# An edge-message layer on one core: two POOL iotas behind every third scatter, from slot 4 to slot 191

## The chip, the cores and the metric

The kernel runs on one core of one Trainium2 chip. The metric is the device time of one execution in microseconds (us). A core has five engines with a queue of instructions each: PE (matrix multiplication), DVE (vector), ACT (scalar, activation), POOL (GpSimd) and SP, which here issues nearly all plain DMA transfers. POOL issues the indirect DMA transfers.

## The reference, cut to what matters

There are 6250 nodes and 100000 edges with 128 features each. Row `src` of an edge is its own node, `dst` its neighbour; the edges come sorted by `dst`.

```python
msg_in = jnp.concatenate([x[row], x[col], edge_attr], axis=-1)
h = msg_in @ W + b
mu = jnp.mean(h, axis=-1, keepdims=True)
var = jnp.mean(jnp.square(h - mu), axis=-1, keepdims=True)
h = (h - mu) * jax.lax.rsqrt(var + LN_EPS) * gamma + beta
msg = jax.nn.relu(h)
out = jax.ops.segment_sum(msg, row, num_segments=x.shape[0])
# edge_index = [src, dst]; the result is _layernorm(x + out)
```

The sum goes by `src`, while the edges lie in the order of `dst`. So the kernel has to bring the rows of one `src` block together, and it does that by writing them, one row for each edge, to computed places in DRAM.

## The kernel before, in words

**Tiles and slots.** The 100000 edges make 782 tiles of 128 edges. Four tiles make a slot `q`, so there are 196 slots (0 to 195). In a slot, PE multiplies the edge features by their part of `W` (L945) and adds the neighbours' projected rows, picked by a one-hot matrix (L962); ACT copies the four finished tiles from PSUM to a row buffer `hs` (L970), and the node number beside them (L971). There are eight such buffers (`HS = 8`), taken in turn: slot `q` uses buffer `q % 8`, so ACT may write it only when the scatters of slot `q - 8` have read it.

**Scatters.** For each tile, POOL issues one indirect DMA (L992), which writes the tile's 128 rows of 528 bytes from `hs` to the places in `place_i` of a DRAM table `sorted`. There are six such tables, one for each part of the edges (`SPLITS`), and 782 scatters in all. From slot 12 on, a scatter also waits for a given matrix product of PE (`TIE`), which spreads a slot's scatters over the next slot. Scatters share eight semaphores in turn (`DMASW0` to `DMASW7`), and each waits for the landing of the scatter eight before it.

**Pairs.** When a part has been scattered, SP loads it back as `hl`, two blocks of 125 nodes at a time (a pair). DVE makes a one-hot matrix of it (L1108), PE turns it (L1120), ACT copies it out (L1124), PE adds the node's own projection (L1147), ACT takes squares and roots (L1156, L1159), DVE scales and cuts (L1171), PE sums by node (L1180), and DVE adds to `acc` (L1198). The pairs of one part are worked on while the next part is scattered.

**The end.** After the last scatter the 25 pairs of the last part remain, and with them the final normalisation, part of which POOL does (L1238, L1239, L1301), and the store.

**Order.** The order on PE, DVE, ACT and SP is written out by hand (`manual_schedule`). POOL's is not while the scatters run: a scheduler places POOL's instructions, and keeps to the dependences between them. A dependence of the kind `NoSync` only orders two instructions, with no semaphore.

The change touches `scatters` (L981 to L1010). It uses `iota_i` (L388), a tile of 128 columns of 32-bit integers that L389 fills once at the start, and that DVE copies to two other tiles (L414, L415); nothing reads it later.

Of the kernel before, what the change touches and what calls it, by code (L numbers as in the profile page):

```python
# [16 lines left out]
P = 128  # L17
# [296 lines left out]
def fast_path(ctx, tc, io, bad_d):  # L314
# [3 lines left out]
    nc = tc.nc  # L318
# [69 lines left out]
    iota_i = const.tile([P, P], I32, name="iota_i")  # L388
# [440 lines left out]
    held = {}  # L829
# [135 lines left out]
    def evict(s, q):  # L965
        t0 = q * PT
        m = min(PT, TILES - t0)
        hs, hp = hs_all[q % HS], held.pop(("hp", q))
        if q > 0:
            nc.scalar.copy(hs[:, :m, 0:D], hp[:, :m, :])  # L970
        nc.scalar.copy(hs[:, :m, D], sloc[:, t0:t0 + m])  # L971
        if q == 0:
            nc.scalar.copy(hs[:, :m, 0:D], hp[:, :m, :])
        waiting.extend((s, q, j) for j in range(m))

    last_scatter = []
    full_scatters = []
    TIE = (12, 196)
    waiting = []

    def scatters(n, tied):  # L981

        total, seen, at = sum(c for _, c in done), 0, []
        for i, c in done:
            seen += c
            while len(at) < n and seen * n >= (len(at) + 1) * total:
                at.append(i)
        done.clear()
        for k, (s, q, j) in enumerate(waiting[:n]):
            t = q * PT + j  # L990
            parts = P if t < TILES - 1 else LAST
            i = nc.gpsimd.indirect_dma_start(  # L992
                out=sorted_d[s][:, :],
                out_offset=bass.IndirectOffsetOnAxis(ap=place_i[:parts, t:t + 1], axis=0),
                in_=hs_all[q % HS][:parts, j, :], in_offset=None,
            )
            last_scatter[:] = [i.ins.name]
            if first_tile[-2] <= t < first_tile[-2] + FULL:
                full_scatters.append(i.ins.name)
            if tied:  # L1000
                tc.add_manual_dep(i.ins, at[k].name, written, reason="rows behind products")
            tc.declare_no_dep(i.ins, group=f"scatter{s}", reason="rows of different edges")
            tc.add_to_no_dep_group(f"scatter{s}", i.ins)
            if t >= first_tile[-2] + FULL:
                tc.declare_no_dep(i.ins, group="halves", reason="see check_full")
                tc.add_to_no_dep_group("behind", i.ins)
            if q < EARLY:
                tc.declare_no_dep(i.ins, group="clear", reason="see check_early")
                tc.add_to_no_dep_group("early", i.ins)
        del waiting[:n]  # L1010
# [314 lines left out]
    for s in range(n_split):  # L1325
        t = first_tile[s]
# [180 lines left out]
    def work(n):  # L1507

        nonlocal n_steps
        for _ in range(n):  # L1510
            for off, step in FLOW:
                i = n_steps - LEAD - off
                if i % 4 or not 0 <= i // 4 < len(pairs):
                    continue
                if step is None:
                    if i // 4 < n_old:
                        load_pair(*pairs[i // 4])
                    continue
                if off == 0:
                    at_work[i // 4] = (Pair if i // 4 < n_old else Unit)(*pairs[i // 4])  # L1520
                step(at_work[i // 4])
            n_steps += 1
# [24 lines left out]
    for s, (n_tiles, _, _, _) in enumerate(SPLITS):  # L1547
        p0, p1 = first_tile[s] // PT, -(-first_tile[s + 1] // PT)
        slots = p1 - p0
        for i in range(slots):  # L1550
            q = p0 + i
# [16 lines left out]
            if q > 2:  # L1568
                evict(s, q)
            if not TIE[0] <= q < TIE[1]:  # L1570
                scatters(len(waiting), False)
            for g in steps_at.pop(q, []):
                run(g)
            work(n - 3)
            if TIE[0] < q < TIE[1]:
                scatters(len(waiting) - PT, True)
# [146 lines left out]
    for key in steps:  # L1723
        if flag is None and starts[key] >= READY["pool"]:
            assert not waiting
            order.enter_context(tc.manual_schedule(engines={mybir.EngineType.Pool}))
            flag = nc.values_load(bad_d[0:1, 0:1], min_val=0, max_val=1 << 20,
                                  skip_runtime_bounds_check_because="a sum of small counts")
        do[key[0]](*key[1:])
        if waiting and key[0] in "KM":  # L1730
            scatters(1, True)
# [6 lines left out]
@with_exitstack  # L1738
def gnn_resnorm_kernel(ctx, tc, io):
    nc = tc.nc  # L1740
    keep = ctx.enter_context(tc.tile_pool(name="keep", bufs=1))
    bad_t = keep.tile([1, 1], I32, name="bad_t")
    with ExitStack() as inner:
        flag = fast_path(inner, tc, io, bad_t)
    with tc.If(flag > 0):
        with ExitStack() as inner:
            general_path(inner, tc, io)
# [244 lines left out]
```

## Time and profile before

| | us |
|---|---|
| time before, median of 3 runs | 1092.25 (1091.75 to 1092.6) |
| the profiled execution's own time | 1092.0 |
| its span, first to last instruction | 1090.2 |
| first scatter starts, last scatter starts | 10.0, 1007.9 |

The profile is of one execution. The page lists for each engine the busy time and its share of the span; its groups of instructions have a row of the form "line engine operation out<-in xcount | busy us, mean ns of one | idle time of the engine just before them, and what ended most of it". The timeline lists instructions by start time with their duration; an idle time before one stands in brackets, with what ended it. "issue" there means that the profile shows nothing that was waited for. Numbers of POOL lines are those of the kernel before.

### The profile page before, as it was taken

How to read it: one execution, taken by the hardware profiler on the slowest of the kernel's cores; microseconds unless marked ns; L12 is line 12 of the kernel's file. 1: busy time of each engine (PE TensorE's matmuls, PEld its weight loads, DVE VectorE, ACT ScalarE, POOL GpSimd, SP SyncE). 2: the span in 40 equal slices, each digit the busy share in tenths (PEclk: the TensorE clock that was granted, in tenths of full speed). 3: DMA queues.
4: the chain of work that ended last, by engine and by line, in shares of the span. 5: the costliest groups of instructions: out<-in, count | busy, mean ns of one | idle time of the engine just before them, and what ended most of it. 6: DMA issues, size and time to landing. Idle time of an engine off the chain costs nothing.

```text
span 1090.2 us, 27196 instructions
## 1 busy us (share of the span) xinstructions
PE 839.6 (77%) x8590; PEld 782.0 (72%) x8590; DVE 876.9 (80%) x2452; ACT 732.4 (67%) x3117; POOL 819.2 (75%) x901
## 2 busy tenths in 40 slices
PE   6366666637887778687787787988879998997995
PEld 5355565527887767587687787988879988896774
DVE  7587998738798888789988876777758887787997
ACT  5133342117666667567666687988879999997796
POOL 7777777777777777777777777777777777777496
PEclk8687797558899898799999998999999999999998
DMA  7899988458787764677877658877859776764572
GB/s 220 263 272 286 303 271 270 147 188 258 227 268 235 237 204 158 222 240 230 266 251 233 188 176 285 284 259 235 259 181 316 231 236 211 229 183 140 151 201 81
DMA packets 127963, 247.92 MB, mean 227 GB/s; under 512 B 47135, under 2 KB 63153, under 8 KB 127813
## 3 DMA queue, kind: packets, MB, share of 16 engines
q1 hardware_dynamic: 101923, 192.81, 58.6%
q0 software_dynamic: 25024, 52.85, 13.5%
q8 instruction: 69, 1.13, 0.4%
q14 instruction: 81, 0.66, 0.2%
q10 hardware_dynamic: 866, 0.46, 0.2%
HBM read 156.23 MB, written 89.80 MB: 226 GB/s over the span
## 4 chain that ended last, share of the span: by engine, by line
PE 28%; DVE 26%; DMA 25%; ACT 13%; issue 5%; SPq 1%; POOL 1%; ACTq 0%; POOLq 0%; DVEq 0%
DMA sorted<-hs,place_i 17%; PE pa L1180 7%; PE hp L945 7%; DVE msg L1171 6%; PE sel L1147 6%; ACT sq L1156 5%; DMA db<-drel_d 5%; DVE sc L695 4%; DVE ohe L1108 3%; ACT sel L1130 3%; ACT ohn L1124 2%; ACT hs L970 2%; PE tr L1120 2%; DVE oh L691 2%; DVE far L714 2%
## 5 line engine op out<-in xcount | busy, mean ns | idle before, releaser
L992 POOL DMA_INDIRECT sorted<-hs,place_i x782 | 757.5, 969 | 241.9 <-issue 88.8
L970 ACT COPY hs<-hp 128x512 f32<-128x512 f32 x194 | 113.0, 583 | 236.3 <-DMA sorted<-hs,place_i 143.3
L1171 DVE SCALAR_TENSOR_TENSOR msg<-sel,rstd,cut 128x128 f32<-128x128 f32 x920 | 260.5, 345 | 8.2
L945 PE MATMUL hp<-w,eT 128*128 128x128 f32 x1548 | 247.2, 310 | 22.4 <-ACT hs L970 19.9
L1147 PE MATMUL sel<-xa,ohn 128*128 128x128 bf16 x2760 | 201.5, 224 | 59.4 <-ACT sel L1130 58.1
L1180 PE MATMUL pa<-msg,ohe 128*128 128x130 f32 x1780 | 239.1, 285 | 5.2 <-DVE msg L1171 2.3
L1156 ACT ACTIVATE sq<-sel 128x128 f32<-128x128 f32 x866 | 227.6, 281 | 18.7 <-PE sel L1147 17.5
L945 PEld LDWEIGHTS hp<-w,eT 128*128 128x128 f32 x1548 | 218.7, 218 | 26.3 <-ACT hs L970 22.6
L1147 PEld LDWEIGHTS <-ohn 128*128 128x128 bf16 x2850 | 183.4, 100 | 71.6 <-issue 52.5
L1180 PEld LDWEIGHTS pa<-msg,ohe 128*128 128x128 f32 x1780 | 217.7, 196 | 9.7 <-PE sel L1147 2.9
L1156 ACT ACTIVATION_READ_ACCUMULATOR sq<-sel 128x1 f32 x866 | 183.4, 212 | 0.0
L1108 DVE TENSOR_TENSOR ohe<-hl,beside 128x1024 f32<-128x1024 f32 (+2 forms) x138 | 138.9, 1007 | 34.2 <-DMA hl<-sorted 33.3
L1130 ACT COPY sel<-hl 128x512 f32<-128x512 f32 (+1 forms) x225 | 127.1, 565 | 35.2 <-DVE msg L1171 29.2
L1124 ACT COPY ohn<-tr 128x1024 bf16<-128x1024 bf16 (+3 forms) x154 | 123.9, 805 | 4.2 <-PE tr L1120 4.1
L934 DVE TENSOR_SCALAR ohd<-db,part_w 128x512 bf16<-128x512 bf16 x192 | 71.6, 373 | 34.3 <-DMA db<-drel_d 26.0
L1120 PE MATMUL tr<-ident_h,ohe 128*128 128x128 bf16 x910 | 76.6, 224 | 19.0 <-DVE ohe L1108 14.2
L1165 DVE RECIPROCAL rstd<-std 128x4 f32<-128x4 f32 (+1 forms) x229 | 39.2, 171 | 59.6 <-ACT std L1159 57.7
L962 PE MATMUL hp<-win,ohd 126*128 126x128 bf16 x770 | 82.5, 234 | 2.8 <-DMA win<-xb_d 2.8
L1198 DVE TENSOR_TENSOR acc<-acc,pa 128x260 f32<-128x260 f32 x123 | 51.6, 419 | 35.3 <-PE pa L1180 34.5
L1120 PEld LDWEIGHTS <-ohe 128*128 128x128 bf16 x910 | 59.1, 100 | 27.8 <-DVE ohe L1108 20.8
L1159 ACT ACTIVATE std<-ss,eps 128x4 f32<-128x4 f32 (+1 forms) x229 | 68.1, 297 | 7.4
L962 PEld LDWEIGHTS <-ohd 126*128 126x128 bf16 x770 | 66.4, 107 | 7.0 <-issue 2.6
(246 smaller groups left out, 862.6 us busy)
## 6 DMA issues: line engine op xcount, KB each, us to landing
eT<-in_eT SPq DMA_DIRECT2D x96, 512.0 KB
hl<-sorted SPq DMA_DIRECT2D x75, 528.0 KB
db<-drel_d SPq DMA_DIRECT2D x96, 256.0 KB
sorted<-empty SPq DMA_DIRECT2D x100, 198.0 KB
sorted<-hs,place_i POOLq DMA_INDIRECT x782
hl<-sorted SPq DMA_DIRECT2D x42, 264.0 KB
hl<-sorted SPq DMA_DIRECT2D x25, 396.0 KB
sorted<-empty SPq DMA_DIRECT2D x50, 132.0 KB
```

What stands on the lines that cost most here:

```text
L945: pe(nc.tensor.matmul(hp[:, j, :], eT[:, at], w[:, 2, :], start=j == 0, stop=False, skip_group_check=True), 4)
L962: pe(nc.tensor.matmul(hp[:, j, :], oh[:3 * WN, at], win[:3 * WN, :], start=False, stop=j == m - 1, skip_group_check=True))
L970: nc.scalar.copy(hs[:, :m, 0:D], hp[:, :m, :])
L992: i = nc.gpsimd.indirect_dma_start(out=sorted_d[s][:, :], out_offset=bass.IndirectOffsetOnAxis(ap=place_i[:parts, t:t + 1], axis=0), in_=h ...
L1108: nc.vector.tensor_tensor(self.ohe[:, :k, :], self.rows()[:, :k, D:D + 1].to_broadcast([P, k, P]), row_bc(iota_p, k), op=ALU.is_equal)
L1120: pe(nc.tensor.transpose(tr[:, j, :], half[:, j0 + j, 1::2], ident_h))
L1124: nc.scalar.copy(self.ohn[:, :self.k, :], self.tr[:, :self.k, :])
L1130: copy(self.sel[g][:, :m, :], self.rows()[:, j0:j0 + m, 0:D])
L1147: pe(nc.tensor.matmul(sel[:, j, :], self.ohn[:, j0 + j, :], xa[:, b, i * D:(i + 1) * D], start=False, stop=j == m - 1 and i == 2, skip_gro ...
L1156: nc.scalar.activation(sq[:, j, :], self.sel[g][:, j, :], AF.Square, accum_out=ss[:, j:j + 1])
L1171: nc.vector.scalar_tensor_tensor(self.msg[:, j0 + j, 0:D], self.sel[g][:, j, :], rstd[:, j:j + 1], cut, op0=ALU.mult, op1=ALU.max)
L1180: pe(nc.tensor.matmul(self.pa[:, h, :], self.ohe[:, j, :], self.msg[:, j, :], start=(j == h), stop=(j == k - 2 + h)), 4)
```

## The change

Behind the scatter of every tile `t` with `t % 3 == 2` in slots 4 to 191, `scatters` issues two iotas on POOL that write 128 columns of `iota_i` in all 128 partitions. Order-only dependences put the first behind that scatter, the second behind the first, and the next scatter in program order behind the second.

```diff
+    PACED = (4, 192)
+    ordered = mybir.DependencyInfo(mybir.DependencyClass.NoSync, mybir.DependencyReason.DATA)
...
         for k, (s, q, j) in enumerate(waiting[:n]):
...
             i = nc.gpsimd.indirect_dma_start(
...
                 in_=hs_all[q % HS][:parts, j, :], in_offset=None,
             )
+            if held.get("pause"):
+                tc.add_manual_dep(i.ins, held.pop("pause"), ordered, reason="behind the pause")
+            if PACED[0] <= q < PACED[1] and t % 3 == 2:
+                last = i.ins.name
+                for _ in range(2):
+                    pause = nc.gpsimd.iota(iota_i, pattern=[[1, P]], base=0, channel_multiplier=0)
+                    tc.add_manual_dep(pause.ins, last, ordered, reason="behind the scatter")
+                    last = pause.ins.name
+                held["pause"] = last
             last_scatter[:] = [i.ins.name]
```

Tiles 17, 20, ... 767 are meant: 251 of them, so 502 iotas. On PE, DVE, ACT and SP the same instructions stand in the same order as before. On POOL the 782 scatters stay, and 502 iotas stand among them: 208 times two in a row, and 86 times one alone.

The usual form is two in a row. Here are POOL's rows near tile 195 (slot 48), before; `sorted1` is the second part's table, `hs0` and `hs1` are row buffers, and the brackets name the semaphores that the instruction waits for: a lane of the scatters' eight, PE's and ACT's.

```order
L992 DMA sorted1_72<-hs0_174,place_i_167 67616x132 [waits DMASW2_49,PE_49]
L992 DMA sorted1_72<-hs0_174,place_i_167 67616x132 [waits DMASW3_49,PE_49]
L992 DMA sorted1_72<-hs1_175,place_i_167 67616x132 [waits DMASW4_49,PE_49,Activation_49]
L992 DMA sorted1_72<-hs1_175,place_i_167 67616x132 [waits DMASW5_49,PE_49]
L992 DMA sorted1_72<-hs1_175,place_i_167 67616x132 [waits DMASW6_49,PE_49]
L992 DMA sorted1_72<-hs1_175,place_i_167 67616x132 [waits DMASW7_49,PE_49]
```

And the same place on POOL in the changed kernel; `x2` is two rows that read alike, and `Pool` is the semaphore that POOL's own instructions count up.

```order
L994 DMA sorted1_72<-hs0_174,place_i_167 67616x132 [waits DMASW2_49,PE_49]
L1004 IOTA iota_i_114 128x128 [waits Pool_49] x2
L994 DMA sorted1_72<-hs0_174,place_i_167 67616x132 [waits DMASW3_49,PE_49]
L994 DMA sorted1_72<-hs1_175,place_i_167 67616x132 [waits DMASW4_49,PE_49,Activation_49]
L994 DMA sorted1_72<-hs1_175,place_i_167 67616x132 [waits DMASW5_49,PE_49]
L1004 IOTA iota_i_114 128x128 [waits Pool_49] x2
L994 DMA sorted1_72<-hs1_175,place_i_167 67616x132 [waits DMASW6_49,PE_49]
L994 DMA sorted1_72<-hs1_175,place_i_167 67616x132 [waits DMASW7_49,PE_49]
```

Two iotas moved in behind every third scatter. All of them write the same tile, and each but the first carries a wait on POOL's own semaphore, for the write of the iota before it.

The other form is rarer. Before, at the turn from slot 45 (`hs5`) to slot 46 (`hs6`) on POOL:

```order
L992 DMA sorted1_72<-hs5_179,place_i_167 67616x132 [waits DMASW4_49,PE_49,Activation_49]
L992 DMA sorted1_72<-hs5_179,place_i_167 67616x132 [waits DMASW5_49,PE_49]
L992 DMA sorted1_72<-hs5_179,place_i_167 67616x132 [waits DMASW6_49,PE_49]
L992 DMA sorted1_72<-hs5_179,place_i_167 67616x132 [waits DMASW7_49,PE_49]
L992 DMA sorted1_72<-hs6_180,place_i_167 67616x132 [waits DMASW0_49,PE_49,Activation_49]
L992 DMA sorted1_72<-hs6_180,place_i_167 67616x132 [waits DMASW1_49,PE_49]
```

And in the changed kernel at that turn:

```order
L994 DMA sorted1_72<-hs5_179,place_i_167 67616x132 [waits DMASW4_49,PE_49,Activation_49]
L1004 IOTA iota_i_114 128x128 [waits Pool_49]
L994 DMA sorted1_72<-hs5_179,place_i_167 67616x132 [waits DMASW5_49]
L994 DMA sorted1_72<-hs5_179,place_i_167 67616x132 [waits DMASW6_49,PE_49]
L1004 IOTA iota_i_114 128x128 [waits Pool_49]
L994 DMA sorted1_72<-hs6_180,place_i_167 67616x132 [waits DMASW7_49,PE_49,Activation_49]
L1004 IOTA iota_i_114 128x128 [waits Pool_49]
L994 DMA sorted1_72<-hs5_179,place_i_167 67616x132 [waits DMASW0_49]
L994 DMA sorted1_72<-hs6_180,place_i_167 67616x132 [waits DMASW1_49,PE_49]
```

Here a scatter stands between the two iotas of a couple, and the last scatter of slot 45 has changed places with the first of slot 46. Five such exchanges of neighbours are all that changes in the order of the 782 scatters.

## The prediction

> **What bounds the kernel now.** I read the page's busy shares first, then POOL's group of scatters, then POOL's timeline.
>
> ```profile
> span 1090.2 us, 27196 instructions
> PE 839.6 (77%) x8590; PEld 782.0 (72%) x8590; DVE 876.9 (80%) x2452; ACT 732.4 (67%) x3117; POOL 819.2 (75%) x901
> ...
> L992 POOL DMA_INDIRECT sorted<-hs,place_i x782 | 757.5, 969 | 241.9 <-issue 88.8
> L970 ACT COPY hs<-hp 128x512 f32<-128x512 f32 x194 | 113.0, 583 | 236.3 <-DMA sorted<-hs,place_i 143.3
> ```
>
> By the shares DVE leads and POOL comes third with 75%. That is misleading. The 782 scatters have 757.5 us of work and 241.9 us of idle time before them, and 241.9 / 782 is 0.31 us for each. The timeline shows what that idle time is:
>
> ```profile
> 402.50 0.96 POOL L992 DMA_INDIRECT sorted<-hs,place_i  x1 [0.30 <-issue]
> 403.76 0.96 POOL L992 DMA_INDIRECT sorted<-hs,place_i  x1 [0.31 <-PE pa L1180]
> 405.02 0.96 POOL L992 DMA_INDIRECT sorted<-hs,place_i  x1 [0.30 <-PE pa L1180]
> ```
>
> Every scatter takes 0.96 us and starts 0.30 us after the one before it ended, whatever engine is named as the releaser. A true wait would vary. So a scatter costs POOL 0.96 + 0.30 = 1.26 us, always, and POOL has no slack. The same in four stages (scatters alone; the columns are the stage, its length, POOL's busy time and the count):
>
> ```profile
> 10.00:260.00 250.00, 188.36 (x193) 0.77 0.82 251
> 260.00:510.00 250.00, 190.22 (x197) 0.90 0.72 227
> 510.00:760.00 250.00, 189.92 (x198) 0.95 0.75 238
> 760.00:1009.00 249.00, 188.97 (x197) 0.97 0.71 221
> ```
>
> 250 / 193 = 1.30, 250 / 197 = 1.27, 250 / 198 = 1.26 and 249 / 197 = 1.26 us a scatter: from 10 us to 1009 us POOL issues scatters back to back, and the only stage with a little room is the first. ACT's copy to `hs` above confirms who waits for whom: of its 236.3 us of idle time, 143.3 end with a scatter's landing. The eight buffers are full, ACT waits for POOL, and PE waits for ACT. **POOL's scatters set the time of the last scatter**, and what follows, 1090.2 - 1008.7 = 81.5 us, is the 25 last pairs, which need the last scatter's rows. A microsecond added to POOL between 60 us and 1009 us is a microsecond at the end; no other engine's cover can hide it.
>
> **The change part by part.** It removes nothing. It adds 502 iotas to POOL: 208 in-a-row couples and 86 single ones. The rows for an iota are at the start of the program, the only ones:
>
> ```profile
> 0.84 0.24 POOL L389 IOTA iota_i<- 128x128 int32 x1 [0.40 <-POOLq L1983]
> 1.03 0.14 POOL L391 IOTA part_i<- 128x1 int32 x1
> 1.11 0.20 POOL masks.py:197 MEMSET ident<- 128x128 f32 x1
> 1.26 0.23 POOL L421 IOTA row_i<- 2x128 int32 x1
> 1.45 0.28 POOL masks.py:199 TENSOR_SCALAR_AFFINE_SELECT ident<-ident 128x128 f32<-128x128 f32 x1
> ```
>
> The very iota of the change lasts 0.24 us, but the next instruction starts 1.03 - 0.84 = 0.19 us after it; the other 128-column iota has 1.45 - 1.26 = 0.19 us too. So 0.19 us is what one takes of POOL when nothing waits for it, and 0.24 us until its write is done.
>
> *A single one* stands between two scatters. Its wait is for an iota at least one scatter (1.26 us) earlier, so it is over when its turn comes: 0.19 us. 86 x 0.19 = 16.3 us.
>
> *Two in a row*: the second waits for the semaphore of the first, that is, for its full 0.24 us and the way of the semaphore. The price of that way is read where POOL's L1239 waits for its own L1238:
>
> ```profile
> 1006.61 0.95 POOL L992 DMA_INDIRECT sorted<-hs,place_i  x1 [0.30 <-ACT std L1159]
> 1007.87 0.87 POOL L992 DMA_INDIRECT sorted<-hs,place_i  x1 [0.30 <-issue]
> 1008.76 0.70 POOL L1238 TENSOR_TENSOR last_y<-acc,g 128x256 f32<-128x256 f32 x1
> 1009.53 0.73 POOL L1239 TENSOR_TENSOR last_y<-last_y,xs 128x256 f32<-128x256 f32 x1
> ```
>
> 1008.76 + 0.70 = 1009.46, and the start is at 1009.53: 0.07 us. So a couple takes 0.24 + 0.07 for the first and 0.19 for the second: 0.50 us. 208 x 0.50 = 104 us. The same rows show that a plain instruction starts 0.02 us after a scatter's end (1007.87 + 0.87 = 1008.74), so nothing is lost on entry. Queued behind the second iota's wait are the next three scatters, which the sums already move.
>
> *The 0.30 us before a scatter* remain, I hold, and come on top; this decides between the forecast and a rival. Two scatters did wait, both for ACT's copy L971:
>
> ```profile
> 42.56 0.20 ACT L971 COPY hs<-sloc 128x4 f32<-128x4 f32 x1
> 58.84 0.20 ACT L971 COPY hs<-sloc 128x4 f32<-128x4 f32 x1
> ...
> 39.64 1.06 POOL L992 DMA_INDIRECT sorted<-hs,place_i  x1 [0.31 <-issue]
> 43.03 0.96 POOL L992 DMA_INDIRECT sorted<-hs,place_i  x1 [2.34 <-ACT hs L971]
> 44.30 0.96 POOL L992 DMA_INDIRECT sorted<-hs,place_i  x1 [0.32 <-issue]
> ...
> 59.31 0.96 POOL L992 DMA_INDIRECT sorted<-hs,place_i  x1 [1.33 <-ACT hs L971]
> ```
>
> POOL had stood idle for 2.34 and 1.33 us, and yet the scatter's recorded start came 0.27 us after the copy's end (43.03 - 42.76, 59.31 - 59.04). So most of the 0.30 us is work at the head of each scatter, not a rest of the one before it; an iota cannot slip into it.
>
> *What is covered*: those two waits. Iotas ahead of 43.03 (some 1.2 us) and between it and 59.31 (more than the 1.0 us by which that wait exceeds 0.30) fill idle time: 2 us off. The five exchanges cost nothing: POOL then runs far behind PE and ACT, and both scatters' data are there. PE, DVE, ACT and SP get no instruction more, and wait longer. The tail starts at the last scatter as before; the last 14 tiles carry no iota, so the distance from the last full tiles to the last scatter is kept.
>
> **Sum** against the profiled execution's own 1092.0 us (its median is 1092.25, which is the same): 1092.0 + 104 + 16 - 2 = **1210 us**, slower by 11%.
>
> Bounds: an iota is worth at least the spacing behind the 128x128 MEMSET (1.26 - 1.11 = 0.15), so a couple 0.24 + 0.07 + 0.15 = 0.46 and the sum 208 x 0.46 + 86 x 0.15 - 3 = 106, 1198 us; and at most its whole 0.24 with 0.09 us for the semaphore, so 0.57, and 208 x 0.57 + 86 x 0.24 = 139, 1231 us. A few us more are possible where DVE's writes hold up POOL's; in the tail, beside a busy DVE, L1239's 0.73 us show none of it.
>
> **A rule weighed.** The Trainium skill ("Perfetto Trace Analysis", GPSIMD Engine Instruction) says to mistrust the span of a POOL instruction and to time it by the spacing of starts. The trace agrees that they differ, 0.24 against 0.19. By that rule alone all 502 are worth 0.19, which is the first rival below. The Trainium skill ("GPSIMD Engine Reference", 2.1 Instruction dispatch) also says that an instruction's completion holds back only what waits on its semaphore; by POOL's order the second iota does wait, and L1239's row agrees.
>
> **The rivals.**
>
> *No hold between the two.* If the second iota does not lose the write and the semaphore, say because the profile's end comes later than the release, all cost 0.19: 502 x 0.19 - 2 = 93, **1185 us**; with 0.15 each, 1165. For it: the spacing rows. Against: L1239 does start only after L1238's end. This is what the spacing rule of the Trainium skill, above, would make of it.
>
> *The iotas hide in the 0.30 us.* Then a single one costs nothing and a couple 0.50 - 0.30 = 0.20: 42 us, **1133 us**. For it: POOL shows as idle there. Against: the 0.27 us after a true wait. The Trainium skill ("Perfetto Trace Analysis", DMA Instruction — SWDGE (GPSIMD)) says that such an instruction has no start marker because it reads no tensor; the two rows agree, in that its shown start is not where its work begins.
>
> *POOL pays for changing over to another kind of work.* The first scatter of all came after a TENSOR_SCALAR and lasted longer:
>
> ```profile
> 10.04 1.22 POOL L992 DMA_INDIRECT sorted<-hs,place_i  x1 [0.66 <-DVE end L761]
> 11.56 0.96 POOL L992 DMA_INDIRECT sorted<-hs,place_i  x1 [0.30 <-DVE hs L833]
> ```
>
> If 1.22 - 0.96 = 0.26 us came back behind each of the 294 groups of iotas, 76 us more: **1286 us**. Against: it may be the first run of that code, and the change over the other way at 1008.76, after 1000 us of nothing else, costs nothing (0.70 us, beside 0.73 for the next).
>
> *Not slower: scatters get shorter by the rest between them.* If a scatter's 0.96 us hold a wait for descriptors or for its DMA queue to drain, a pause would shorten the three that follow. From 0.50 / 3 = 0.17 us (17% of a scatter) each, it pays for itself: **1092 us**, and below that beyond. Against: the scatter after 2.34 us of idle time still took 0.96, and so did the one after 1.33.
>
> That the iotas might not be there, or be dropped, is excluded by POOL's order above.
>
> **How the numbers follow.** The forecast has 0.62, no hold 0.22, hiding 0.06, the change-over 0.06, shorter scatters 0.04. The range is 1170 to 1238: it holds the forecast's bounds with some us for contention above, and nearly all of the no-hold case, together some 0.84; the others are left out. A measurement of this kernel can tell about 0.2% from no change. All cases but the last are slower by more: 0.96. The last I split into 0.03 for no difference and 0.01 for faster.
>
> **What would show it.** In the profile after: 782 scatters still of 0.96 us; between the third scatter of a triple and the next 0.30 + 0.50 = 0.80 us instead of 0.30, with two iotas in it, 0.31 us apart from start to start; the last scatter's start near 1126 us; ACT's waits for scatters far above 143.3 us; the stretch behind the last scatter still near 81 us. Two iotas 0.19 us apart say no hold; a scatter that starts within 0.1 us of an iota says hiding; scatters of 1.2 us behind iotas say change-over. The forecast is wrong in its base if POOL shows idle time that changes with its releaser, for then something else had set the pace.

## The result, and the profile after

The changed kernel takes 1267.06 us (median of 3 runs, 1266.44 to 1267.96), against 1092.25 us before: 1.159 times as long, with a 95% interval of 1.157 to 1.161. The forecast was 1210 us, with a range up to 1238. The direction and the place were right, the size was not: 175 us came where 118 were forecast.

These are the rows of the page of the changed kernel that answer to those of before; L994 is the scatter, which was L992, and L1004 is the iota.

```profile
span 1265.3 us, 27662 instructions
PE 892.1 (71%) x8590; PEld 832.9 (66%) x8590; DVE 880.8 (70%) x2452; ACT 735.2 (58%) x3117; POOL 951.7 (75%) x1403
...
L994 POOL DMA_INDIRECT sorted<-hs,place_i x782 | 765.0, 978 | 265.9 <-issue 149.2
L970 ACT COPY hs<-hp 128x512 f32<-128x512 f32 x194 | 113.3, 584 | 401.8 <-DMA sorted<-hs,place_i 321.1
...
L945 PE MATMUL hp<-w,eT 128*128 128x128 f32 x1548 | 264.0, 324 | 57.5 <-ACT hs L970 55.9
...
L1004 POOL IOTA iota_i<- 128x128 int32 x502 | 124.7, 248 | 18.2
```

DVE and ACT have the busy time that they had, and POOL has 132.5 us more. PE has 52.5 us more as well, with the same instructions: its granted clock was 0.853 in this execution and 0.900 in the one before, and a product of L945 took 324 ns instead of 310. PE also waits more (55.9 us for ACT ahead of L945, where it was 19.9). The extra time is POOL's all the same, as the last scatter's start shows below. ACT's waits for a scatter's landing went from 143.3 to 321.1 us: the row buffers are full for longer. POOL's rows account for the whole: 124.7 us of iotas, 18.2 us idle before them, 24.0 us more idle before scatters and 7.5 us more in the scatters make 174.4 us. What the page doesn't show is how the price is shared out, for the 24.0 us mix scatters that have less than the usual 0.30 us before them with scatters that have more. One has to look at the two kinds apart, in POOL's timeline (start, duration, and in brackets the idle time before; two iotas in a row are merged into one row, which goes from the start of the first to the end of the second and names the first one's width alone):

```profile
531.28 0.96 POOL L994 DMA_INDIRECT sorted<-hs,place_i  x1 [0.30 <-PE pa L1191]
532.24 0.56 POOL L1004 IOTA iota_i<- 128x128 int32 x2
533.27 0.98 POOL L994 DMA_INDIRECT sorted<-hs,place_i  x1 [0.47 <-PE tr L1131]
534.56 0.96 POOL L994 DMA_INDIRECT sorted<-hs,place_i  x1 [0.30 <-issue]
535.82 0.96 POOL L994 DMA_INDIRECT sorted<-hs,place_i  x1 [0.30 <-ACT sel L1141]
536.79 0.26 POOL L1004 IOTA iota_i<- 128x128 int32 x1
537.22 0.98 POOL L994 DMA_INDIRECT sorted<-hs,place_i  x1 [0.17 <-issue]
538.23 0.25 POOL L1004 IOTA iota_i<- 128x128 int32 x1
538.65 0.98 POOL L994 DMA_INDIRECT sorted<-hs,place_i  x1 [0.17 <-issue]
539.94 0.96 POOL L994 DMA_INDIRECT sorted<-hs,place_i  x1 [0.30 <-issue]
```

Behind a single iota the scatter starts 0.17 us after it, less than the usual 0.30: 537.22 + 1.26 would be 538.48 without the iota, and it is 538.65. So a single one costs 0.17 here; by the medians from scatter to scatter over the run, 1.424 against 1.263 us before, 0.16. Behind two in a row the scatter starts 0.47 us after the second, and the way from the scatter ahead to it is 533.27 - 531.28 = 1.99 instead of 1.26 us: **0.73 us for a couple**, where the prediction had 0.50. In the median of the 208 couples it is 1.997 us, the same. 208 x 0.73 = 152, 86 x 0.16 = 14, and the scatter behind iotas lasts 0.98 instead of 0.96, 294 x 0.02 = 6: 172 us. The last scatter starts at 1181.5 instead of 1007.9, 173.6 us later, and behind it come 1265.3 - 1182.4 = 82.9 us, where there were 81.5. So PE's slower products can have cost little more than these 1.4 us.

### The profile page after: what moved, and what is told of

Same layout as the page of the kernel before. It is cut to its first block, busy times and chain, and to the rows that moved or that the text cites. A ratio compares the mean times of both kernels' runs of the same rounds, so it can differ in the third digit from the quotient of the medians.

```text
span 1265.3 us, 27662 instructions
## 1 busy us (share of the span) xinstructions
PE 892.1 (71%) x8590; PEld 832.9 (66%) x8590; DVE 880.8 (70%) x2452; ACT 735.2 (58%) x3117; POOL 951.7 (75%) x1403
## 4 chain that ended last, share of the span: by engine, by line
PE 29%; DMA 22%; DVE 16%; POOL 11%; ACT 11%; issue 9%; SPq 1%; POOLq 0%; ACTq 0%; DVEq 0%
DMA sorted<-hs,place_i 16%; POOL sorted L994 9%; PE pa L1191 9%; PE hp L945 8%; PE sel L1158 6%; ACT sq L1167 4%; DMA db<-drel_d 3%; DVE msg L1182 3%; DVE sc L695 3%; ACT sel L1141 2%; ACT hs L970 2%; POOL iota_i L1004 2%; PE hp L962 2%; PE tr L1131 2%; DVE ohe L1119 2%
## 5 line engine op out<-in xcount | busy, mean ns | idle before, releaser
L994 POOL DMA_INDIRECT sorted<-hs,place_i x782 | 765.0, 978 | 265.9 <-issue 149.2
L970 ACT COPY hs<-hp 128x512 f32<-128x512 f32 x194 | 113.3, 584 | 401.8 <-DMA sorted<-hs,place_i 321.1
L1158 PE MATMUL sel<-xa,ohn 128*128 128x128 bf16 x2760 | 209.9, 229 | 134.4 <-ACT sel L1141 133.7
L945 PE MATMUL hp<-w,eT 128*128 128x128 f32 x1548 | 264.0, 324 | 57.5 <-ACT hs L970 55.9
L1158 PEld LDWEIGHTS <-ohn 128*128 128x128 bf16 x2850 | 191.6, 103 | 149.2 <-issue 118.4
L945 PEld LDWEIGHTS hp<-w,eT 128*128 128x128 f32 x1548 | 233.2, 230 | 62.7 <-ACT hs L970 60.2
L1191 PE MATMUL pa<-msg,ohe 128*128 128x130 f32 x1780 | 256.2, 299 | 5.0 <-DVE msg L1182 2.9
L1191 PEld LDWEIGHTS pa<-msg,ohe 128*128 128x128 f32 x1780 | 235.7, 210 | 8.7 <-PE sel L1158 3.6
L1176 DVE RECIPROCAL rstd<-std 128x4 f32<-128x4 f32 (+1 forms) x229 | 39.5, 172 | 148.0 <-ACT std L1170 147.5
L1004 POOL IOTA iota_i<- 128x128 int32 x502 | 124.7, 248 | 18.2
L962 PE MATMUL hp<-win,ohd 126*128 126x128 bf16 x770 | 87.4, 244 | 3.2 <-DMA win<-xb_d 3.2
L962 PEld LDWEIGHTS <-ohd 126*128 126x128 bf16 x770 | 70.6, 112 | 8.4 <-issue 3.2
```

Of the source, the lines that this page charges most:

```text
L945: pe(nc.tensor.matmul(hp[:, j, :], eT[:, at], w[:, 2, :], start=j == 0, stop=False, skip_group_check=True), 4)
L962: pe(nc.tensor.matmul(hp[:, j, :], oh[:3 * WN, at], win[:3 * WN, :], start=False, stop=j == m - 1, skip_group_check=True))
L994: i = nc.gpsimd.indirect_dma_start(out=sorted_d[s][:, :], out_offset=bass.IndirectOffsetOnAxis(ap=place_i[:parts, t:t + 1], axis=0), in_=h ...
L1004: pause = nc.gpsimd.iota(iota_i, pattern=[[1, P]], base=0, channel_multiplier=0)
L1158: pe(nc.tensor.matmul(sel[:, j, :], self.ohn[:, j0 + j, :], xa[:, b, i * D:(i + 1) * D], start=False, stop=j == m - 1 and i == 2, skip_gro ...
L1191: pe(nc.tensor.matmul(self.pa[:, h, :], self.ohe[:, j, :], self.msg[:, j, :], start=(j == h), stop=(j == k - 2 + h)), 4)
```

## The experiments

**Two theories** of the 0.23 us that a couple costs beyond its forecast. *Late preparation*: while the second iota is held by its semaphore, nothing behind it on POOL's queue can be made ready. Before, the queue ran ahead of the work and had the next scatters ready. Behind a held iota it begins only when the iota leaves, and the scatter comes a fixed time after the first iota's end, whatever the second one does meanwhile. *Change-over*: two iotas in a row cost the scatter behind them 0.2 us by themselves, and all terms add. The kernels below change the loop that issues the iotas and nothing else, except for the tile that they write.

**e1_two_tiles**: the second iota writes another tile that is not needed any more, and is not held.

```diff
-                for _ in range(2):
-                    pause = nc.gpsimd.iota(iota_i, pattern=[[1, P]], base=0, channel_multiplier=0)
+                for pause_i in (iota_i, iota_row.bitcast(I32)):
+                    pause = nc.gpsimd.iota(pause_i, pattern=[[1, P]], base=0, channel_multiplier=0)
```

> Same 502 iotas, 251 times two in a row, but the two write different tiles, so the second no longer waits for the first. Theory 'late preparation' (while the second iota is held, POOL's queue cannot begin to prepare the next scatter, which takes it some 0.77 us from the first iota's end): no hold, so a couple costs 0.01 + 0.25 + 0.19 + 0.17 - 0.30 + 0.02 = 0.34 us more than no iota, 251 x 0.34 = 85, about 1175 us; the scatter starts 0.17 us after the second iota. Rival 'change-over' (two iotas in a row cost the next scatter 0.2 us by themselves): only the hold of 0.12 us goes, 251 x 0.61 = 153, about 1243 us; the scatter still starts 0.47 us after the second iota.

Measured: 1179.5 us (1.079 times before, 1.076 to 1.083). POOL's timeline of e1_two_tiles:

```profile
499.44 0.96 POOL L994 DMA_INDIRECT sorted<-hs,place_i  x1 [0.30 <-issue]
500.41 0.25 POOL L1004 IOTA iota_i<- 128x128 int32 x1
500.60 0.25 POOL L1004 IOTA iota_row<- 128x128 int32 x1
501.02 0.98 POOL L994 DMA_INDIRECT sorted<-hs,place_i  x1 [0.17 <-issue]
```

The second starts 0.19 us after the first, before its end, and the scatter 0.17 us after the second. With the hold, 88 us of the 175 are gone, though the same 502 iotas run, 251 times two in a row. Change-over falls.

**e2_short_second**, **e3_long_second**: the second iota has 1 column, or 256, instead of 128, and stays held. For 256 columns `iota_i` and the tile behind it became one tile `wide_i`.

```diff
-                for _ in range(2):
-                    pause = nc.gpsimd.iota(iota_i, pattern=[[1, P]], base=0, channel_multiplier=0)
+                for width in (P, 1):
+                    pause = nc.gpsimd.iota(iota_i[:, :width], pattern=[[1, width]], base=0, channel_multiplier=0)
```

> The second iota writes 1 column instead of 128 and still waits for the first. Late preparation: the scatter still starts 0.77 us after the first iota's end, whatever stands between, so the 208 couples cost the same, and only the 43 short ones that stand alone get cheaper by 0.1: 1263 us. Rival 'change-over, all terms add': 251 x 0.1 = 25 us less, 1242 us.

> The second iota writes 256 columns instead of 128 and still waits for the first. Late preparation: its 0.11 us more lie beside the preparation, so the couples cost the same; only the some 46 that stand alone cost 0.11 more: 1272 us. Rival 'all terms add': 251 x 0.107 = 27 us more, 1294 us.

Measured: 1263.6 us with 1 column (1.157, 1.154 to 1.159) and 1267.6 us with 256 (1.161, 1.157 to 1.164): nearly the 1267.1 with 128, within 5 us of late preparation's figures, and 22 and 26 us from what added terms give. POOL's timeline, first of e2_short_second, then of e3_long_second:

```profile
502.04 0.95 POOL L994 DMA_INDIRECT sorted<-hs,place_i  x1 [0.30 <-issue]
503.00 0.46 POOL L1004 IOTA iota_i<- 128x128 int32 x2
504.02 0.99 POOL L994 DMA_INDIRECT sorted<-hs,place_i  x1 [0.57 <-issue]
```

```profile
547.72 0.95 POOL L995 DMA_INDIRECT sorted<-hs,place_i  x1 [0.30 <-issue]
548.68 0.67 POOL L1005 IOTA wide_i<- 128x128 int32 x2
549.71 0.98 POOL L995 DMA_INDIRECT sorted<-hs,place_i  x1 [0.36 <-PE sel L1160]
```

The idle time before the scatter went from 0.47 to 0.57 and to 0.36, and made up for the second iota's length to 0.01 us: from the start of the first iota to the scatter it is 1.02 and 1.03 us, against 533.27 - 532.24 = 1.03 in the changed kernel.

**e6_both_short**: both iotas have 1 column, so that they write a 128th, but the hold is whole.

```diff
-                    pause = nc.gpsimd.iota(iota_i, pattern=[[1, P]], base=0, channel_multiplier=0)
+                    pause = nc.gpsimd.iota(iota_i[:, :1], pattern=[[1, 1]], base=0, channel_multiplier=0)
```

> Both iotas write 1 column; the second waits for the first. Nearly no work is left, the hold is whole. Late preparation: first iota 0.14, then 0.77 to the scatter, so 0.01 + 0.14 + 0.77 - 0.30 + 0.02 = 0.64 us a couple, 211 x 0.64 + 80 x 0.06 = 140, about 1230 us. Rival 'change-over': 0.14 + 0.07 + 0.08 + 0.2 - 0.1 = 0.39, about 1180 us. The prediction's sum (0.14 + 0.07 + 0.08 = 0.29 a couple): about 1158 us.

Measured: 1239.9 us (1.135, 1.131 to 1.138). That is 10 us over late preparation's figure and 60 over change-over's. From scatter to scatter a couple takes 1.89 us in the median, 0.63 more than before, where late preparation had 0.64: the 10 us lie outside the couples, and where was not found out. POOL's timeline of e6_both_short:

```profile
500.35 0.35 POOL L1004 IOTA iota_i<- 128x1 int32 x2
501.27 0.99 POOL L994 DMA_INDIRECT sorted<-hs,place_i  x1 [0.57 <-issue]
```

From start to scatter it is 0.92 us, 0.11 less than with 128 columns, which is by how much the first iota got shorter. In all four kernels with a hold, the changed one among them, the median time from the first iota's end to the scatter's start is 0.77 us (208, 208, 205 and 211 couples); without it, in e1, 0.36. An iota of 1 column still lasts 0.14 us, against 0.25. So what the 502 iotas write makes little of the time: with a 128th of it, 147 us of 175 remain.

**e10_spread_last**, **e11_one_last**: single iotas. e10 has the same 502, one behind each of two scatters of three, and each still waits for the one before, but a scatter stands between. e11 has one behind every third.

```diff
-            if PACED[0] <= q < PACED[1] and t % 3 == 2:
+            if PACED[0] <= q < PACED[1] and t % 3 > 0:
...
-                for _ in range(2):
+                for _ in range(1):
```

> 502 single iotas once more, for a chip on which the kernel before takes some 1092 us: late preparation 502 x 0.16 - 2 = 78 more, about 1170 us; if the iotas' work and number cost, 1267 us. Where the kernel before takes some 1335 to 1355 us: no difference.

> 251 single iotas, on the same chip. Where the kernel before takes some 1092 us: late preparation about 1130 us, the prediction's price 1138 us, the count of iotas 1180 us. Where it takes some 1335 to 1355 us: no difference.

Measured: 1171.2 us (1.073, 1.069 to 1.076) and 1131.7 us (1.036, 1.033 to 1.040), 0.16 us for an iota in both (79 / 502, 39.5 / 251). POOL's timeline of e10_spread_last:

```profile
502.26 0.25 POOL L1004 IOTA iota_i<- 128x128 int32 x1
502.69 0.98 POOL L994 DMA_INDIRECT sorted<-hs,place_i  x1 [0.17 <-issue]
503.68 0.26 POOL L1004 IOTA iota_i<- 128x128 int32 x1
504.11 0.98 POOL L994 DMA_INDIRECT sorted<-hs,place_i  x1 [0.17 <-PE pa L1191]
```

The same work and the same dependences, moved one scatter apart, cost 79 us instead of 175. POOL's queue is held here too: the semaphore instruction that belongs to the scatter of 504.11 ran at 502.56, 0.04 us after the end of the iota for which the iota of 503.68 waits. But a scatter and an iota lie between, so that it still ran 1.55 us ahead of its own scatter, and POOL itself didn't wait.

**Runs where POOL is not the bound.** The two kernels of single iotas had been run before, and fell on chips on which the kernel before itself took some 1335 to 1355 us.

> One iota instead of two behind every third scatter, 251 in all, none held by the one before. Late preparation: each costs what a single one costs in the changed kernel, 0.16 us, so 251 x 0.16 - 2 = 38, about 1130 us. The prediction's price of 0.19: 1138 us. If the time went by the count of iotas: half of the 175 us, 1180 us.

> The same 502 iotas, but one each behind two of every three scatters, never two in a row; each still waits for the one before, over one scatter at least. Late preparation: 502 x 0.16 - 2 = 78, about 1170 us. If it is the iotas' work and number that cost: 1267 us as in the changed kernel.

| run | us | before, same chip | ratio (95% interval) |
|---|---|---|---|
| e4_one | 1356.3 | 1355.7 | 1.001 (0.998 to 1.003) |
| e5_spread | 1356.6 | 1355.7 | 1.001 (0.999 to 1.004) |
| e4_one_again | 1353.0 | 1352.9 | 0.999 (0.997 to 1.002) |
| e5_spread_again | 1355.1 | 1352.9 | 1.001 (0.999 to 1.004) |
| e4_one_third | 1356.2 | 1354.3 | 1.001 (0.999 to 1.004) |
| e5_spread_third | 1355.4 | 1354.3 | 1.001 (0.998 to 1.004) |
| e5_spread_fourth | 1334.2 | 1337.2 | 0.997 (0.994 to 1.001) |
| e8_after_profiled (the changed kernel) | 1351.4 | 1350.6 | 1.001 (0.997 to 1.004) |
| e9_spread_beside | 1354.0 | 1350.6 | 1.003 (1.000 to 1.006) |

They could not tell the price of an iota. But they raised a question of their own, for which the unchanged and the changed kernel ran side by side on such a chip (e7_before_profiled, e8_after_profiled, e9_spread_beside).

> The kernel before, for its profile beside the next two on the same chip. Where it takes some 1092 us: scatters 1.26 us apart throughout. Where it takes some 1340 to 1355 us: POOL waits between scatters for other engines, in total some 250 us more idle time than the 242 us of the profile before.

> The changed kernel beside the kernel before on this chip. Where the kernel before takes some 1092 us: 1267 us again. Where it takes some 1340 to 1355 us: its last scatter starts near 1258 us there, and the couples need POOL only until about 1182 us, so most of their 170 us fall into waits: within 2% of the kernel before by either theory of the couple's price, as long as the cost is one of POOL's time and not of anything else.

> 502 single iotas. Where the kernel before takes some 1092 us: late preparation 1170 us, count of iotas 1267 us. Where it takes some 1340 to 1355 us: no difference.

First the engines of the chain that ended last in the profile before, at 1092 us; then a part of the page of e7_before_profiled, the same kernel, and a stretch of its POOL timeline; then the scatter's row of e8_after_profiled:

```profile
PE 28%; DVE 26%; DMA 25%; ACT 13%; issue 5%; SPq 1%; POOL 1%; ACTq 0%; POOLq 0%; DVEq 0%
```

```profile
PE 52%; DVE 20%; issue 16%; another core or an unknown queue 6%; ACT 5%; SPq 1%; DMA 0%; POOL 0%; ACTq 0%; DVEq 0%; POOLq 0%
...
L992 POOL DMA_INDIRECT sorted<-hs,place_i x782 | 754.7, 965 | 491.0 <-issue 236.9
...
L1147 PE MATMUL sel<-xa,ohn 128*128 128x128 bf16 x2760 | 232.9, 233 | 101.4 <-issue 83.2
```

```profile
601.18 0.96 POOL L992 DMA_INDIRECT sorted<-hs,place_i  x1 [0.30 <-issue]
603.23 0.96 POOL L992 DMA_INDIRECT sorted<-hs,place_i  x1 [1.10 <-PE sel L1147]
604.84 0.96 POOL L992 DMA_INDIRECT sorted<-hs,place_i  x1 [0.65 <-PE pa L1180]
606.26 0.96 POOL L992 DMA_INDIRECT sorted<-hs,place_i  x1 [0.46 <-ACT hs L971]
```

```profile
L994 POOL DMA_INDIRECT sorted<-hs,place_i x782 | 763.3, 976 | 339.9 <-issue 170.6
```

Here the idle time before scatters does vary with its releaser, and comes to 491.0 us instead of 241.9. PE leads the chain that ended last, with 52%. In the profile before, DMA had 25% of the span on it, 17% for the landings of scatters alone; here DMA and POOL have 0%. PE itself stands idle for reasons that its rows only call "issue" (83.2 us before L1147, where the profile before has 59.4 us in all, nearly all of it for ACT). The changed kernel puts its iotas and its holds into these waits (491.0 fell to 339.9), the couples have their usual form (a median of 2.01 us from scatter to scatter), and the time is the same to 0.4%, some 5 us. So the change costs POOL's time: the full 175 us where POOL sets the pace, and none that can be told from the spread of the runs where it waits. Why PE starves on those chips wasn't found out.

## Why the prediction was wrong

- **What bounds the kernel** was right. The even 0.30 us before each scatter meant that POOL never waits, and each microsecond given to POOL came out at the end: 173.6 us at the last scatter, 175 in the time. The runs on the other chips are the counter-test, which the prediction had named: idle time that changes with its releaser, and then no cost.
- **The single iota**: 0.19 forecast, 0.16 measured. "An iota cannot slip into it" was too strict: 0.13 of the scatter's 0.30 us do lie beside the iota ahead of it (0.17 remain), of which 0.02 come back in the scatter. On 86 of them that is 2 us.
- **The hold** was seen, and was the right reason not to take the no-hold rival: the second starts 0.07 us after the first's end, to the digit of L1239's row. e1, which is that rival made into a kernel, took 1179.5 us, near its 1185.
- **The step that failed** is the sentence on what stands behind the hold: "Queued behind the second iota's wait are the next three scatters, which the sums already move." The sum let the scatter follow the second iota by 0.19 + 0.30 = 0.49 us from start to start, as if it had been waiting ready behind it. It hadn't. 0.77 us pass from the first iota's end to the scatter, 0.07 of hold and 0.70 from there, instead of 0.07 + 0.49. That is 0.21 of the 0.23 us missing for a couple, some 44 of the 57 us; the longer scatters behind iotas (6 us) and a sum of small parts are the rest.
- **The mechanism of it**, late preparation, is shown in what it does: the fixed 0.77 us through four lengths of work, and its absence without the hold.
- **The queue itself** shows it too. On it, each scatter has a semaphore instruction of its own, for the landing of the scatter eight before. How long this runs ahead of its scatter's start is the queue's lead (all times here are medians). In the unchanged kernel the lead is 5.8 us, more than four scatters. Behind a held couple it is 0.73 us: the semaphore instruction runs 0.04 us after the first iota's end, and the following one 0.52 us later, 0.21 us before the scatter starts; this in all four kernels. In e1, behind a couple without a hold, the lead is 4.26 us. For the second and the third scatter behind a held couple it is 1.50 and 2.24 us, so the queue wins some 0.75 us back with each scatter of 1.26 us. It thus spends about half a microsecond on one scatter, which is hidden as long as it is ahead. The unchanged kernel agrees: from 60 us on, a fifth of the intervals between these instructions are 0.50 to 0.53 us, and nearly none is shorter (3 of 740). What the queue does in that time, no run shows. The Trainium skill ("Perfetto Trace Analysis", DMA Instruction — SWDGE (GPSIMD)) has an instruction pass a wait queue, and move on to the cores that work it off only when its semaphores are satisfied. The trace agrees for the held iota, which starts 0.07 us after the first one's end, and adds what the hold costs the scatter behind it.
- The other rivals fell. Hiding would have left 1133, and only 0.13 us of the head can be shared. Change-over gave 0.02 us, not 0.26, behind every group. Scatters did not get shorter by the rest (0.98 behind iotas, 0.96 otherwise).
- The bounds were too narrow for the same reason: above, they let the iota and its semaphore grow, but kept the scatter's start behind it.

## What to carry to other kernels

Idle time that is the same before each instruction, whatever releases it, can be part of the instruction: here it was, and POOL was busy throughout, while shares of busy time would have named DVE. On an engine that sets the pace, an instruction that waits for the one just ahead of it can cost more than the wait: here it also took away the queue's lead, and the 0.5 us that the queue needs for the next scatter came into the open. Put a scatter's worth of work between the two, or let them write different tiles, and the same work costs half (79 and 86 us of 175).

## What the runs showed of the hardware that had not been expected

A POOL iota held by the one ahead delays the scatter to 0.77 us after the first one's end, whether the second writes 1, 128 or 256 columns; unheld, the scatter starts 0.17 us after the second one's end. A scatter behind an iota lasts 0.98 us instead of 0.96. POOL's queue was about 5.8 us ahead of POOL in the unchanged kernel, and needs about 0.5 us for a scatter. And one unchanged program took 1092 us on some chips and 1337 to 1356 us on others (medians), in every run there, with PE idle for no reason that the profile shows.
